# An expert's gate and up products in seven block products for eight, and its gathered rows moved inside the chip

## The chip, the cores and the metric

One core of a Trainium2 chip runs the whole program. The time is the device time of one execution, in microseconds. Three runs of the kernel before took 678.39 to 678.44 us, with a median of 678.43. TensorE (PE) multiplies matrices, VectorE (DVE), ScalarE (ACT) and GpSimd (POOL) work on elements, SyncE (SP) issues most transfers, and POOL issues the indirect ones. PEld is the loading of weights into PE.

## The reference

A layer on 8 sequences of 256 tokens with 512 features, in float32. An attention in the form of a long convolution comes first; the change does not touch it. Then each of the 2048 tokens chooses 4 of 16 experts, and every expert works on at most 256 tokens:

```python
xg = xpad[buf]                                   # 16 experts x 256 tokens x 512
gact = silu(einsum('ech,ehi->eci', xg, w_gate))  # 512 -> 352
mid = gact * einsum('ech,ehi->eci', xg, w_up)
eout = einsum('eci,eih->ech', mid, w_down) * wbuf[..., None]
y = zeros((T + 1, h)).at[buf.reshape(-1)].add(eout.reshape(-1, h))[:T]
shared = silu(x @ sw_gate) * (x @ sw_up) @ sw_down
x + y + shared
```

## The kernel before, in words

The first 340 us hold the attention, with the shared expert's blocks filled in between (`shared_block`, L142 to L197); the rest of these blocks runs until 419 us, while the routing is worked out. From there on the loop over the 16 experts has PE to itself. Constants: P = 128, NC = 4 chunks of the 512 features, CAP = 256 tokens in NSL = 2 halves of 128, NB = 4 blocks of 32, I = 352 = 2 x 128 + 96, so NW = 2 whole feature tiles and a tail of 96. AHEAD = 3 is how many experts the loop looks ahead.

Every engine works through its instructions in the order of the program (a manual schedule); nothing is moved by a planner. Semaphores hold the dependences between engines. For expert e the loop issues:

- `gate_up` (L1023): first the tail. Its gate and up columns lie packed in `wt`; L1046 and L1054 multiply them with the tokens `xgT`, and three rounds of an ACT operation (L1063 twice, L1067) and a DVE multiplication (L1064 twice, L1068) give its part of `mid`. These rounds use one tile in turn, so ACT and DVE alternate. Then for each of the two whole feature tiles f, gate and up with 4 chunks each: 16 products with 256 tokens as columns (L1034) in all. ACT takes the silu of gate out of PSUM (L1041), DVE multiplies by up from PSUM (L1042).
- `pack(e+1)` (L1011), two copies on ACT, and `tokens(e+1)` (L998): two copies of the routing weights (L1003) and two block transposes of 32 x 32 (L404) on DVE. They turn the rows in `gb` into `xgT`, features on the partitions.
- `find(e+3)` (L915): PE finds the expert's tokens from the comparison made earlier (L920), and seven small DVE operations (L928 to L943) form the index lists. Then `gather(e+3)` (L974): two indirect transfers on POOL (L977) fetch 256 rows into `g`.
- `down` (L1076) for n = 0 and n = 1: six products (tail, f = 0, f = 1, of both halves; L1080 at 512 columns), DVE scales the result by the routing weight on its way out of PSUM (L1088), and POOL adds the rows to `out` with an indirect transfer (L1091), after a small memset (L1090).
- `compare(e+4)` (L904): one DVE comparison of 2048 elements a partition, with both inputs in SBUF (L907).
- `load_expert(e+3)` (L852): four transfers on SP, 2.2 MB of weights, into the buffers that expert e leaves. Then `shuffle(e+3)` (L985): the gathered rows are written to a DRAM tile `slots` (L989), and four transfers of 32 partitions each read them back as `gb` (L992), in the order that the block transposes want: partition b of block i holds the features of block i, of the rows b of every block j.

Expert 15 is done in halves of 128 tokens, so that its first half can leave while the second is multiplied. `xnT` (L103, 32 KB a partition) holds the normalised tokens for the shared expert; after the last shared block nothing reads it. `ps_mm` and `ps_tr` are the PSUM pools of that part, two buffers each, free in the expert loop; the loop's own pool `ps_ex` has three.

Of the kernel before, what the change touches and what calls it, by code (L numbers as in the profile page):

```python
# [8 lines left out]
F32 = mybir.dt.float32  # L9
BF16 = mybir.dt.bfloat16  # L10
I32 = mybir.dt.int32
AF = mybir.ActivationFunctionType
# [8 lines left out]
P = 128  # L21
BK = 32
B, S, L = 8, 256, 512
# [7 lines left out]
E, K, CAP, I, IS = 16, 4, 256, 352, 704  # L31
NSL = CAP // P
NB = P // BK
# [20 lines left out]
def ssm_attention__then__moe_kernel(  # L54
# [22 lines left out]
    nc = tc.nc  # L77
# [25 lines left out]
    xnT = keep.tile([P, NC, NT, P], F32, name="xnT")  # L103
# [156 lines left out]
    with ExitStack() as att:  # L260
# [16 lines left out]
            out=exch,  # L277
            in_=exch,
# [386 lines left out]
        def stir(count):  # L665
# [7 lines left out]
            out=skip_b,  # L673
            in_=bass.AP(tensor=skip.tensor, offset=skip.offset + FIRST * HT, ap=[[0, P], [1, HT]]),
# [164 lines left out]
    ffn = ctx.enter_context(tc.tile_pool(name="ffn", bufs=2))  # L839
# [6 lines left out]
    AHEAD = 3  # L846
# [5 lines left out]
    def load_expert(e):  # L852
        if e % AHEAD < AHEAD - 1:
            w = wpool.tile([P, 2, NC, I], F32, name="w")
            wd = wpool.tile([P, NI, L], F32, name="wd")
        else:
            w, wd = old_w, old_wd
        full = I // P * P
        nc.sync.dma_start(out=w[:, 0], in_=w_gate[e].rearrange("(p c) f -> p c f", p=P))
        nc.sync.dma_start(out=w[:, 1], in_=w_up[e].rearrange("(p c) f -> p c f", p=P))  # L860
        nc.sync.dma_start(
            out=wd[:, 0 : I // P, :], in_=w_down[e, 0:full, :].rearrange("(c p) f -> p c f", p=P)
        )
        nc.sync.dma_start(out=wd[0 : I - full, I // P, :], in_=w_down[e, full:, :])
        return w, wd
# [79 lines left out]
    experts = {e: load_expert(e) for e in range(AHEAD)}  # L945
# [39 lines left out]
    def shuffle(g):  # L985


        slots = dram.tile([CAP, L], F32, name="slots", bufs=2)
        nc.sync.dma_start(out=slots.rearrange("(n q) f -> q n f", n=NSL), in_=g[:, :, 0:L])  # L989
        gb = ffn.tile([P, NSL * NB, P], F32, name="gb", bufs=AHEAD - 1)  # L990
        for i in range(NB):
            nc.sync.dma_start(  # L992
                out=gb[i * BK : (i + 1) * BK],
                in_=slots[:, i * P : (i + 1) * P].rearrange("(j b) f -> b j f", b=BK),
            )
        return gb

    def tokens(e):  # L998

        gb, g = moved.pop(e), gathered.pop(e)  # L1000
        wg = ffn.tile([P, NSL], F32, name="wg")
        for n in range(NSL):
            nc.vector.tensor_copy(wg[:, n : n + 1], g[:, n, L + e : L + e + 1])  # L1003
        xgT = ffn.tile([P, NC, CAP], F32, name="xgT")
        for n in range(NSL):
            transpose_blocks(xgT[:, :, n * P : (n + 1) * P], gb[:, n * NB : (n + 1) * NB])
        return xgT, wg

    NW, Q = I // P, P // 4
# [13 lines left out]
    def gate_up(xgT, mid, w, wt, cols, fs=(I // P, *range(I // P))):  # L1023

        halves = range(cols.start // P, cols.stop // P)
        for f in fs:
            pgu = ps_ex.tile([P, 2, CAP], F32, name="pgu", tag="ex")
            act = ffn.tile([P, CAP], F32, name="eact")  # L1030
            if f < NW:
                for k in range(2):
                    for c in range(NC):
                        nc.tensor.matmul(  # L1034
                            pgu[:, k, cols],
                            lhsT=w[:, k, c, f * P : (f + 1) * P],
                            rhs=xgT[:, c, cols],
                            start=(c == 0),
                            stop=(c == NC - 1),
                        )  # L1040
                nc.scalar.activation(act[:, cols], pgu[:, 0, cols], AF.Silu)  # L1041
                nc.vector.tensor_mul(mid[:, f, cols], act[:, cols], pgu[:, 1, cols])  # L1042
                continue
            for c in range(NC):
                for n in halves:
                    nc.tensor.matmul(  # L1046
                        pgu[2 * Q * n : 2 * Q * (n + 1), 1, 0:P],
                        lhsT=wt[:, c, P:],
                        rhs=xgT[:, c, n * P : (n + 1) * P],
                        start=(c == 0),  # L1050
                        stop=(c == NC - 1),
                    )
            for c in range(NC):
                nc.tensor.matmul(  # L1054
                    pgu[:, 0, cols],
                    lhsT=wt[:, c, 0:P],
                    rhs=xgT[:, c, cols],
                    start=(c == 0),
                    stop=(c == NC - 1),
                )  # L1060
# [12 lines left out]
    between = route.tile([P, 1], F32, name="between")  # L1073
    SYNC = mybir.DependencyInfo(mybir.DependencyClass.Sync, mybir.DependencyReason.DATA)

    def down(e, n, mid, wd, wg):  # L1076
        po = ps_ex.tile([P, L], F32, name="eo", tag="ex")
        for k, f in enumerate((NW, *range(NW))):
            m = min(P, I - f * P)
            nc.tensor.matmul(  # L1080
                po,
                lhsT=mid[:m, f, n * P : (n + 1) * P],
                rhs=wd[:m, f, :],
                start=(k == 0),
                stop=(k == NW),
            )
# [12 lines left out]

        done = done.ins  # L1100
        scattered.append(done)
        if e > 0:
            if n == 1:
# [9 lines left out]
    xgT_next = tokens(0)  # L1113
# [5 lines left out]
    for e in range(E):  # L1119
        w, wd = experts.pop(e)  # L1120
        wt = wt_next
        xgT, wg = xgT_next
        mid = ffn.tile([P, NI, CAP], F32, name="mid")
        if e + 1 < E:
            gate_up(xgT, mid, w, wt, slice(0, CAP))
            wt_next = pack(experts[e + 1][0])
            xgT_next = tokens(e + 1)
            if e + AHEAD < E:
                find(e + AHEAD, hots.pop(e + AHEAD))
                gathered[e + AHEAD] = gather(e + AHEAD)  # L1130
            for n in range(NSL):
                down(e, n, mid, wd, wg)
            if e + AHEAD + 1 < E:
                hots[e + AHEAD + 1] = compare(e + AHEAD + 1)
        else:

            gate_up(xgT, mid, w, wt, slice(0, P))
            gate_up(xgT, mid, w, wt, slice(P, CAP), (NW,))
            down(e, 0, mid, wd, wg)
            gate_up(xgT, mid, w, wt, slice(P, CAP), range(NW))  # L1140
            down(e, 1, mid, wd, wg)
        if e + AHEAD < E:
            experts[e + AHEAD] = load_expert(e + AHEAD)
            moved[e + AHEAD] = shuffle(gathered[e + AHEAD])
# [38 lines left out]
```

## Time and profile before

| what | value |
|---|---|
| median of three runs | 678.43 us |
| the profiled execution | 678.52 us |
| its span | 676.8 us |
| granted PE clock over the span | 0.995 |
| PE busy | 654.2 us, 97% |
| PEld busy | 486.9 us, 72% |
| DVE busy | 385.8 us, 57% |
| POOL busy | 320.2 us, 47% |
| ACT busy | 184.2 us, 27% |
| 11 loads of `w` by gate, 11 by up, 5 and 5 into the old tile `xs` | 704 KB each |
| L1034, 256 columns, 480 instructions | 106.0 us busy, mean 379 ns |
| L907 comparison on DVE, 16 | 36.5 us busy, mean 2281 ns |
| L977 gathers on POOL, 32 | 34.9 us busy, mean 1092 ns |
| L1091 scatters on POOL, 32 | 59.5 us busy, mean 1859 ns |

A line of the timeline or of the chain has the start and the length in microseconds, the engine, the line of the kernel, the operation and its tiles, the shape and how many instructions were merged; in brackets stands how long the engine idled before it and what ended that. PE's instructions overlap their predecessor's, so the mean of one (379 ns) is longer than the distance to the next; what a product costs in a stream is read from start to start. A float32 product of the program is two PE instructions.

### The profile page before, as it was taken

Reading aid. Unit: us, or ns where it says so; the run is one execution under the profiler, and the core shown is the slowest. Engines: PE = TensorE matmul, PEld = TensorE weight load, DVE = VectorE, ACT = ScalarE, POOL = GpSimd, SP = SyncE. Lnnn points to the kernel's source line nnn. Section 1 sums busy time; section 2 is a strip of 40 time slices with the busy share of each in tenths; the row PEclk is TensorE's granted clock in tenths of the full one; section 3 lists DMA queues with packets and bytes.
Section 4 is the critical chain, followed back from the end, with each engine's and each line's share of the span. In section 5 each row is a group of like instructions: output and inputs, shape, how many; then the busy total and the mean of one; then the engine's idle time right before and its main releaser. Section 6 shows DMA issues by size and latency. Waiting matters only on the chain.

```text
span 676.8 us, 9807 instructions
## 1 busy us (share of the span) xinstructions
PE 654.2 (97%) x3321; PEld 486.9 (72%) x3321; DVE 385.8 (57%) x932; ACT 184.2 (27%) x465; POOL 320.2 (47%) x509
## 2 busy tenths in 40 slices
PE   6899999998999999999999999999999999999994
PEld 5687877777867877876867685777776667777772
DVE  4956576878877776767536621444445545553231
ACT  2464533444342343313332010111121111111110
POOL 5677646877685777547120320243333444443111
PEclk9999999999999999999999999999999999999998
DMA  5793455555557536351008672588888889999822
GB/s 131 237 269 105 125 151 145 145 140 140 147 141 188 134 94 161 103 133 46 16 23 298 198 234 64 169 267 255 259 269 269 256 258 270 271 266 273 248 32 31
DMA packets 98439, 117.79 MB, mean 174 GB/s; under 512 B 11268, under 2 KB 64356, under 8 KB 98389
## 3 DMA queue, kind: packets, MB, share of 16 engines
q1 hardware_dynamic: 90932, 99.86, 48.9%
q0 software_dynamic: 7168, 17.04, 12.1%
q10 hardware_dynamic: 288, 0.26, 0.3%
q8 instruction: 26, 0.43, 0.3%
q14 instruction: 25, 0.20, 0.1%
HBM read 84.25 MB, written 32.88 MB: 173 GB/s over the span
## 4 chain that ended last, share of the span: by engine, by line
PE 85%; DVE 4%; DMA 3%; issue 2%; POOL 2%; ACT 2%; SPq 1%; POOLq 0%; DVEq 0%; ACTq 0%
PE sgu L168 20%; PE pgu L1034 15%; PE y L468 15%; PE eo L1080 12%; PE so L185 11%; PE pgu L1054 4%; PE pgu L1046 2%; PE sgt L154 2%; PE shared L468 2%; PE ip L920 1%; PE pt L529 1%; POOL kv L445 1%; DMA xs<-in_x 1%; DMA out<-eo_sb,idx 1%; DVE y L517 1%
## 5 line engine op out<-in xcount | busy, mean ns | idle before, releaser
L468 PE MATMUL y<-kv,toep 128*128 128x288 f32 x528 | 138.7, 407 | 4.8 <-DVE f L518 3.0
L468 PEld LDWEIGHTS y<-kv,toep 128*128 128x128 f32 x528 | 98.9, 190 | 35.4 <-issue 7.1
L977 POOL DMA_INDIRECT g<-xw_d,ido x32 | 34.9, 1092 | 170.8 <-DVE idx L943 132.3
L520 POOL TENSOR_TENSOR f<-f 128x256 f32<-128x256 f32 x60 | 43.8, 730 | 90.2 <-DVE f L518 85.0
L445 POOL TENSOR_TENSOR kv<-k 128x256 f32<-128x256 f32 x126 | 85.1, 707 | 0.0
L1091 POOL DMA_INDIRECT out<-eo_sb,idx x32 | 59.5, 1859 | 46.1 <-DVE eo_sb L1088 35.4
L168 PE MATMUL sgu<-xnT,swg 128*128 128x256 f32 (+1 forms) x400 | 78.1, 338 | 0.4 <-DVE tail L162 0.4
L1034 PE MATMUL pgu<-xgT,w 128*128 128x256 f32 (+1 forms) x384 | 78.2, 362 | 0.0
L168 PE MATMUL sgu<-xnT,swu 128*128 128x256 f32 (+1 forms) x400 | 77.9, 338 | 0.0
L1034 PEld LDWEIGHTS pgu<-xgT,w 128*128 128x128 f32 x384 | 68.2, 190 | 8.7 <-issue 0.5
L185 PE MATMUL so<-swd,smid 128*128 128x512 f32 x160 | 73.9, 593 | 0.0
L168 PEld LDWEIGHTS sgu<-xnT,swg 128*128 128x128 f32 x400 | 65.3, 191 | 7.9 <-DVE tail L162 0.6
L168 PEld LDWEIGHTS sgu<-xnT,swu 128*128 128x128 f32 x400 | 64.6, 191 | 6.3
L1080 PE MATMUL eo<-wd,mid 96*128 96x512 f32 (+1 forms) x132 | 59.4, 598 | 0.0
L1042 DVE TENSOR_TENSOR mid<-eact,pgu 128x256 f32<-128x256 f32 (+1 forms) x34 | 13.8, 406 | 77.6 <-ACT eact L1041 77.6
L491 DVE TENSOR_TENSOR y<-y,again 128x576 f32<-128x576 f32 x28 | 21.4, 766 | 57.8 <-PE y L468 48.1
L185 PEld LDWEIGHTS so<-swd,smid 128*128 128x128 f32 x160 | 29.9, 190 | 31.9 <-issue 30.4
L177 ACT ACTIVATE act<-sgu 128x256 f32<-128x256 f32 (+1 forms) x50 | 17.1, 341 | 121.6 <-PE sgu L168 121.6
L518 DVE TENSOR_TENSOR f<-y,z 128x512 f32<-128x512 f32 x64 | 44.3, 692 | 6.6 <-DVE y L517 0.5
L517 DVE TENSOR_TENSOR y<-y,q 128x512 f32<-128x512 f32 x64 | 44.8, 700 | 2.2
L1063 ACT ACTIVATE eact<-pgu 32x128 f32<-32x128 f32 x32 | 8.5, 267 | 129.0 <-PE pgu L1054 123.8
L1080 PEld LDWEIGHTS eo<-wd,mid 96*128 96x128 f32 (+1 forms) x132 | 24.1, 189 | 26.0 <-issue 23.5
(178 smaller groups left out, 928.2 us busy)
## 6 DMA issues: line engine op xcount, KB each, us to landing
toep<-win_d SPq DMA_DIRECT2D x28, 320.0 KB
slots<-g SPq DMA_DIRECT2D x16, 512.0 KB
gb<-slots SPq DMA_DIRECT2D x64, 128.0 KB
w<-in_L_ffn_w_gate SPq DMA_DIRECT2D x11, 704.0 KB
w<-in_L_ffn_w_up SPq DMA_DIRECT2D x11, 704.0 KB
got<-sent SPq DMA_DIRECT2D x26, 256.0 KB
wd<-in_L_ffn_w_down SPq DMA_DIRECT2D x11, 512.0 KB
xs<-in_x SPq DMA_DIRECT2D x16, 256.0 KB
```

Source lines behind the costliest of these rows:

```text
L168: nc.tensor.matmul(pgu[:, k, :], lhsT=sw[:, c, f * P : (f + 1) * P], rhs=toks[:, c, :], start=(c == 0), stop=(c == NC - 1),)
L185: nc.tensor.matmul(po, lhsT=m[:, i * P : (i + 1) * P], rhs=swd[:, (f - 1) % (NF + 1), :], start=(f == 0), stop=(f == NF),)
L445: (nc.vector if c in helped else nc.gpsimd).tensor_mul(kv[:, c, 0 : ND * HB].rearrange("p (d w) -> p d w", d=ND), kh[:, c, 0:HB].unsqueeze ...
L468: nc.tensor.matmul(out, lhsT=toep[:, m * P : (m + 1) * P], rhs=rhs, start=(n == 0), stop=(n == len(pairs) - 1),)
L517: nc.vector.tensor_mul(yd, yd, view(qq, 0, [[qc, 2], [B, ND], [1, HB]]))
L518: nc.vector.tensor_add(f, yd, z[:, :, :, BACK : BACK + HB])
L520: adder.tensor_add(f[:, :, 0:2, :], f[:, :, 0:2, :], f[:, :, 2:4, :])
L977: nc.gpsimd.indirect_dma_start(out=g[:, n, :], out_offset=None, in_=xw_d[:, :], in_offset=bass.IndirectOffsetOnAxis(ap=ido[:, e, n : n + 1 ...
L1034: nc.tensor.matmul(pgu[:, k, cols], lhsT=w[:, k, c, f * P : (f + 1) * P], rhs=xgT[:, c, cols], start=(c == 0), stop=(c == NC - 1),)
L1054: nc.tensor.matmul(pgu[:, 0, cols], lhsT=wt[:, c, 0:P], rhs=xgT[:, c, cols], start=(c == 0), stop=(c == NC - 1),)
L1080: nc.tensor.matmul(po, lhsT=mid[:m, f, n * P : (n + 1) * P], rhs=wd[:m, f, :], start=(k == 0), stop=(k == NW),)
L1091: done = nc.gpsimd.indirect_dma_start(out=out, out_offset=bass.IndirectOffsetOnAxis(ap=idx[:, e, n : n + 1], axis=0), in_=o, in_offset=Non ...
```

## The change

`shuffle` no longer goes through DRAM. Sixteen transfers from SBUF to SBUF, one for each pair of a block j of rows and a block i of features, bring the rows from `g` to `gb`, whose layout gets the halves on the outside.

For experts 1 to 14 the two whole feature tiles of gate and up are no longer multiplied in the plain way. The 512 features are halved into k = 0, 1 (two chunks each), the outputs into gate and up, the 256 tokens into two halves of 128. In these 2 x 2 x 2 blocks the plain way has eight block products; `strassen` forms seven, of 8 instructions with 128 columns each for a block of two feature tiles and two chunks (7 x 2 x 2 = 28 products, 56 PE instructions, for 16 products and 32 instructions with 256 columns). What it needs besides:

- `weight_sums(e+1)`: four POOL operations of 512 elements a partition on the next expert's weights, at the head of iteration e.
- `token_sums(e+1)`: four DVE operations of 256 elements on the next expert's tokens, behind `tokens(e+1)`.
- In `strassen`: two ACT copies out of PSUM and two silu operations, and seven DVE operations: two additions into `u2` and two into `u3` with one input in PSUM, one addition and two multiplications with both inputs in SBUF.

The sums and intermediate results lie in `xnT`, two sets for two experts. Four PSUM tiles of `ps_mm` and `ps_tr` take the products. The tail and expert 0 and 15 stay as they were. `down` takes the second half (n = 1) ahead of the first. The diff, cut to its core:

```diff
     def shuffle(g):
-        slots = dram.tile([CAP, L], F32, name="slots", bufs=2)
-        nc.sync.dma_start(out=slots.rearrange("(n q) f -> q n f", n=NSL), in_=g[:, :, 0:L])
-        gb = ffn.tile([P, NSL * NB, P], F32, name="gb", bufs=AHEAD - 1)
-        for i in range(NB):
-            nc.sync.dma_start(
-                out=gb[i * BK : (i + 1) * BK],
-                in_=slots[:, i * P : (i + 1) * P].rearrange("(j b) f -> b j f", b=BK),
-            )
+        gb = ffn.tile([P, NSL, NB, P], F32, name="gb", bufs=AHEAD - 1)
+        for j in range(NB):
+            for i in range(NB):
+                nc.sync.dma_start(
+                    out=gb[i * BK : (i + 1) * BK, :, j, :],
+                    in_=g[j * BK : (j + 1) * BK, :, i * P : (i + 1) * P],
+                )
         return gb
...
+    def weight_sums(e, w):
+        (a11, a12), (a21, a22) = blocks_of(w)
...
+        nc.gpsimd.tensor_add(sums[0], a21, a22)
+        nc.gpsimd.tensor_sub(sums[1], sums[0], a11)
+        nc.gpsimd.tensor_sub(sums[2], a11, a21)
+        nc.gpsimd.tensor_sub(sums[3], a12, sums[1])
+        return sums
+
+    def token_sums(e, xgT):
...
+        nc.vector.tensor_sub(sums[0], b12, b11)
+        nc.vector.tensor_sub(sums[1], b22, sums[0])
+        nc.vector.tensor_sub(sums[2], b22, b12)
+        nc.vector.tensor_sub(sums[3], b21, sums[1])
+        return sums
+
+    def strassen(xgT, mid, w, s, t):
...
+        product(0, a11, b11)
+        nc.scalar.copy(p1, ps[0])
+        product(1, s[1], t[1])
+        nc.vector.tensor_add(u2, ps[1], p1)
+        product(2, s[0], t[0])
+        nc.scalar.copy(p5, ps[2])
+        product(0, a12, b21)
+        nc.scalar.activation(act0, ps[0], AF.Silu)
+        product(2, s[3], b22)
+        nc.vector.tensor_add(u2, ps[2], u2)
+        nc.scalar.activation(act1, u2, AF.Silu)
+        product(1, s[2], t[2])
+        nc.vector.tensor_add(u3, ps[1], p1)
+        nc.vector.tensor_add(p5, u3, p5)
+        nc.vector.tensor_mul(mid[:, 0:NW, P : 2 * P], act1, p5)
+        product(3, a22, t[3])
+        nc.vector.tensor_add(u3, ps[3], u3)
+        nc.vector.tensor_mul(mid[:, 0:NW, 0:P], act0, u3)
...
         mid = ffn.tile([P, NI, CAP], F32, name="mid")
+        if e + 2 < E:
+            s_next = weight_sums(e + 1, experts[e + 1][0])
         if e + 1 < E:
-            gate_up(xgT, mid, w, wt, slice(0, CAP))
+            if e == 0:
+                gate_up(xgT, mid, w, wt, slice(0, CAP))
+            else:
+                gate_up(xgT, mid, w, wt, slice(0, CAP), (NW,))
+                strassen(xgT, mid, w, sums, token_sums_now)
             wt_next = pack(experts[e + 1][0])
             xgT_next = tokens(e + 1)
+            if e + 2 < E:
+                sums, token_sums_now = s_next, token_sums(e + 1, xgT_next[0])
             if e + AHEAD < E:
                 find(e + AHEAD, hots.pop(e + AHEAD))
                 gathered[e + AHEAD] = gather(e + AHEAD)
-            for n in range(NSL):
+            for n in reversed(range(NSL)):
                 down(e, n, mid, wd, wg)
```

Products 0 and 3 of the second round add to what the same PSUM tile already holds. In the changed kernel the product is at L1132, the POOL sums at L1095 to L1098, the token sums at L1111 to L1114, ACT's copies at L1147 and L1151, DVE's operations at L1149, L1155, L1158, L1159, L1160, L1162 and L1163, and the down products at L1169.

More of the change, by code (lines that the diff above doesn't have):

```diff
@@ L1005, in tokens @@
         for n in range(NSL):
-            transpose_blocks(xgT[:, :, n * P : (n + 1) * P], gb[:, n * NB : (n + 1) * NB])
+            transpose_blocks(xgT[:, :, n * P : (n + 1) * P], gb[:, n])
         return xgT, wg
@@ L1074, in ssm_attention__then__moe_kernel, with spare, blocks_of @@
     SYNC = mybir.DependencyInfo(mybir.DependencyClass.Sync, mybir.DependencyReason.DATA)
+    F = NW * P
+    free = xnT.rearrange("p c n q -> p (c n q)")
+    def spare(at, n):
+        return free[:, at : at + n]
+    def blocks_of(w):
+        return [[w[:, m, 2 * k : 2 * k + 2, 0:F] for k in range(2)] for m in range(2)]
+    def weight_sums(e, w):
+        (a11, a12), (a21, a22) = blocks_of(w)
+        sums = [
+            spare((e % 2 * 4 + i) * 2 * F, 2 * F).rearrange("p (c f) -> p c f", c=2)
+            for i in range(4)
+        ]
+        nc.gpsimd.tensor_add(sums[0], a21, a22)
[3 more added lines that the diff above has]
+        return sums
@@ new lines, in token_sums @@
+    def token_sums(e, xgT):
+        (b11, b12), (b21, b22) = [
+            [xgT[:, 2 * k : 2 * k + 2, n * P : (n + 1) * P] for n in range(2)] for k in range(2)
+        ]
+        at = 16 * F
+        sums = [
+            spare(at + (e % 2 * 4 + i) * 2 * P, 2 * P).rearrange("p (c q) -> p c q", c=2)
+            for i in range(4)
+        ]
+        nc.vector.tensor_sub(sums[0], b12, b11)
[3 more added lines that the diff above has]
+        return sums
@@ new lines, in strassen, with product, place @@
+    def strassen(xgT, mid, w, s, t):
+        (a11, a12), (a21, a22) = blocks_of(w)
+        (b11, b12), (b21, b22) = [
+            [xgT[:, 2 * k : 2 * k + 2, n * P : (n + 1) * P] for n in range(2)] for k in range(2)
+        ]
+        ps = [
+            pool.tile([P, NW, P], F32, name=f"gu{i}", tag=tag)
+            for i, (pool, tag) in enumerate(((ps_mm, "mm"), (ps_mm, "mm"), (ps_tr, "pt"), (ps_tr, "pt")))
+        ]
+        begun = set()
+        def product(i, a, b):
+            for f in range(NW):
+                for c in range(2):
+                    nc.tensor.matmul(
+                        ps[i][:, f, :],
+                        lhsT=a[:, c, f * P : (f + 1) * P],
+                        rhs=b[:, c, :],
+                        start=(i not in begun),
+                        stop=(c == 1),
+                        skip_group_check=True,
+                    )
+                    begun.add(i)
+        def place(i):
+            return spare(16 * F + 16 * P + i * F, F).rearrange("p (f q) -> p f q", f=NW)
+        p1, p5, u2, u3, act0, act1 = (place(i) for i in range(6))
+        product(0, a11, b11)
[16 more added lines that the diff above has]
+        nc.vector.tensor_mul(mid[:, 0:NW, 0:P], act0, u3)
@@ L1102, in down @@
         if e > 0:
-            if n == 1:
+            if len(scattered) % 2 == 0:
                 tc.declare_no_dep(done, scattered[2 * e], reason="other rows of out")
```

## The prediction

> **What bounds the kernel now.** I read the chain of work first. Its shares by engine and by line:
>
> ```profile
> PE 85%; DVE 4%; DMA 3%; issue 2%; POOL 2%; ACT 2%; SPq 1%; POOLq 0%; DVEq 0%; ACTq 0%
> PE sgu L168 20%; PE pgu L1034 15%; PE y L468 15%; PE eo L1080 12%; PE so L185 11%; PE pgu L1054 4%; PE pgu L1046 2%; PE sgt L154 2%; PE shared L468 2%; PE ip L920 1%; PE pt L529 1%; POOL kv L445 1%; DMA xs<-in_x 1%; DMA out<-eo_sb,idx 1%; DVE y L517 1%
> ```
>
> The change touches the expert loop, 419 us to the end. Next, the chain in order of time there (start, length, what), one expert:
>
> ```profile
> 512.30 1.02 PE pgu L1046 x16
> 513.32 1.92 PE pgu L1054 x8
> 515.25 6.91 PE pgu L1034 x32
> 522.15 0.38 PE ip L920 x16
> 522.53 5.26 PE eo L1080 x12
> ```
>
> 1.02 + 1.92 + 6.91 + 0.38 + 5.26 = 15.49 us per expert, and the next begins at 527.79: PE never waits. A matrix product of the program is two PE instructions (16 calls of L1034 are x32). Busy time in the stretch of eight such experts (PE, PEld, DVE, ACT, POOL, clock, DMA share, GB/s) shows what is near PE:
>
> ```profile
> 496.80:620.80 124.00, 124.00 (x674) 88.33 (x676) 61.08 (x152) 19.92 (x56) 49.65 (x48) 1.00 0.92 274
> ```
>
> Per expert DVE 7.6 us, POOL 6.2, ACT 2.5, so each has room by its mean. DVE's waits in the stretch are for PE or ACT, PE's for nothing.
>
> **PE's gain.** The timeline gives the price of both widths: 256 columns before, 128 in the last expert, which is cut in halves already.
>
> ```profile
> 515.08 7.07 PE L1034 MATMUL pgu<-xgT,w 128*128 128x256 f32 x32
> 521.99 0.54 PE L920 MATMUL ip<-what,hot 128*128 128x6 bf16 x16
> ...
> 661.01 3.73 PE L1034 MATMUL pgu<-xgT,w 128*128 128x128 f32 x32
> 664.58 2.74 PE L1080 MATMUL eo<-wd,mid 96*128 96x512 f32 x6
> ```
>
> From start to next start, (521.99 - 515.08)/32 = 0.216 us and (664.58 - 661.01)/32 = 0.1116 us. Seven products of 8 instructions are 56 x 0.1116 = 6.25 us for 6.91: 0.66 less. Experts 1 to 14 take the new way, so 14 x 0.66 = 9.2 us if PE goes on unhindered, at 14.84 us per expert.
>
> **DVE's chain without collisions.** DVE gains five operations in the products (seven, L1149 to L1163, in place of the two multiplications L1042; the tail's three stay: 5 x 0.42 = 2.1 us) and four token sums (L960, same size, both inputs in SBUF: 0.424; 1.6 us together). They form a ring, since DVE runs in order and the next expert's PE needs it back:
> - From the sixth product in PSUM: add, add, multiply, add, multiply, 2.1; copies of the weights and two transposes, 1.34 (538.53 to 539.86 before); token sums 1.6; the seven small index operations 1.0; two evictions 1.34; the comparison L907 2.2. Together 9.6.
> - Then the next tail: three multiplications alternating with ACT, then ACT's copy of p1, which the fourth product waits for because it writes the same PSUM: 0.28 + 0.31 + 0.32 + 0.42 + 0.38 + 0.19 to PE = 1.9.
> - Products four to six: 3 x 0.894, and 0.2 until DVE sees them: 2.9.
>
> 14.4 us, under PE's 14.84. So this alone hides, with 0.4 us of slack.
>
> **POOL's sums and the shared port.** POOL gets four operations of 512 elements per expert. L520 and L521 on POOL (adds) took 0.730 us for 256 elements and 0.459 for 128, 2.12 ns an element, so 512 are about 1.28 us. The multiplications L445 and L443 give 1.2 as the low bound; 1.4 is the high one (strided operands). Mean time allows 5.1 us: POOL 6.2 + 5.1 of 15. But the trace shows what DVE operations with both inputs in SBUF do beside such work. At 32 us POOL idles, at 15 us it multiplies:
>
> ```profile
> 15.22 0.72 DVE L520 TENSOR_TENSOR f<-f 128x256 f32<-128x256 f32 x1
> 15.61 0.89 POOL L445 TENSOR_TENSOR kv<-k 128x256 f32<-128x256 f32 x1
> 15.97 0.67 DVE L521 TENSOR_TENSOR oT<-f 128x128 f32<-128x128 f32 x1
> ...
> 32.28 0.42 DVE L520 TENSOR_TENSOR f<-f 128x256 f32<-128x256 f32 x1
> 32.74 0.29 DVE L521 TENSOR_TENSOR oT<-f 128x128 f32<-128x128 f32 x1
> ```
>
> L521 took 0.67 for 0.29: it ends 0.29 after 16.35, and POOL ended at 16.50. POOL's own 0.89 for 0.70 is the same the other way. They take turns, each beginning about 0.14 before the other's end. The Trainium skill (SBUF — State Buffer, Who interferes with whom) has the rule: a DVE instruction with two SBUF inputs and a GpSimd instruction that reads SBUF exclude each other for the whole instruction; one with a PSUM input does not. The row agrees except for those 0.14 us of overlap; L518 (one input in PSUM) stays at 692 ns beside a busy POOL. POOL's indirect transfers are held too, by the comparison:
>
> ```profile
> 381.89 2.28 DVE L907 TENSOR_TENSOR hot<-pos,slot_f 128x2048 bf16<-128x2048 f32 x1
> 382.77 2.50 POOL L977 DMA_INDIRECT g<-xw_d,ido  x1 [27.72 <-DMA xw_d<-prob]
> 385.57 0.97 POOL L977 DMA_INDIRECT g<-xw_d,ido  x1 [0.30 <-issue]
> ```
>
> **Where they meet.** POOL's order is gather, gather, scatter, scatter, four sums for the expert after the next. The first gather goes when DVE has the index; the second is held by the comparison and ends 1.1 us after it; 0.3 + 1.93 + 1.6 for the scatters: the sums begin about 4.9 us after the comparison's end. DVE's first add of two SBUF operands (into p5) wants to begin 1.9 + 2.9 + 0.45 = 5.25 after the same end. So it finds the first sum 0.35 us old and waits 1.28 - 0.35 - 0.14 = 0.8. The second sum takes the port as it ends; the multiplication behind it waits 1.28 - 0.31 = 0.95; the last multiplication comes 0.37 after that one and waits 0.6; the fourth sum falls beside the transposes, which have one input (705 ns where POOL is busy, 686 here). The waits are 2.35 us, the ring is 14.4 + 2.35 = 16.8. PE feels it twice: the down product of the second half waits for its mid, and the fourth product for p1. Who else is queued: the gathers behind the sums have 6 us and more before a transfer is missed. By the rule without the 0.14 the waits are 0.7 longer and the end 11 x 0.7 = 8 us later (700); I take the row.
>
> Sum: experts 2 to 12, 11 x (16.78 - 15.50) = +14.1; expert 1 about even (its ring begins undelayed), -0.1; expert 13, with no comparison behind it but sums still to come, +0.95; expert 14, no sums, -0.65. Together +14.3. The profiled execution took 678.52 us (span 676.8; the 1.7 around it stay), the median of the runs is 678.43: 678.5 + 14.3 = 692.8.
>
> **The direct transfers.** The write of 512 KB to DRAM goes, and five issues become sixteen. SP waited 73.4 us in eight experts for the write to land, yet nobody waited for SP: one wait of 1.5 us for gb in all. So I cost it at nothing. 16 x 0.45 (four gb issues took 1.80) + 1.7 for the weights = 8.9 us of SP per expert, under 15; the next weights are queued behind, needed more than an expert later. Packets are 512 bytes as in the reads before. Low bound 0 gain, since no wait is there to go; high bound, if gb came an expert's slack (6 us at the last one) too late, some us once. The reversed order of the halves (its first half is the one finished first), the first expert's unchanged products and the PE waits for sums on hand a whole expert ahead cost nothing while the ring lets them.
>
> **Rivals.**
> - The exclusion hardly bites (sums shorter, or falling into DVE's other work): 678.5 - 9.2 = 669.3, faster. It decides from waits under 15.5 - 14.4 = 1.1 us per expert. For it: POOL is free 9 of 15 us. Against: the sums follow the same comparison as DVE's adds, so the phase repeats. 10%.
> - Half of it: POOL's transfers are not held as I think, or an operation costs 1.0: one or two waits remain, ring 14.9 to 15.8, 672 to 683. 13%.
> - Worse: sums of 1.4 us and more, token sums caught too, or gb late: 699 to 710. 5%.
> - The forecast: 683 to 698 with its bounds (1.2 us per sum +10.7, 1.4 +19), 72%.
>
> The measurement can tell about 0.2% (1.4 us). Faster: 10 and most of half of the 13, 0.17; same 0.04; slower 0.79. The range leaves out the clean gain, the lower part of the half case and the worst: 678 to 699.
>
> **What would show it.** Right: L1132 at 112 ns from start to start; PE idle before it and before eo, ended by ACT or DVE; the DVE lines L1159, L1160 and L1163 at 0.8 to 1.4 us for 0.42; POOL sums at 1.28 and more; experts 16.8 us apart. Wrong: those DVE lines at 0.42 and experts 14.84 apart, or waits for gb or w on PE.

## The result and the profile after

The changed kernel took 698.04 us, the median of four runs (696.66 to 698.61), against 678.43 before: 1.0286 times as long, with an interval of 1.0274 to 1.0299. The profiled execution took 696.66 us, with a span of 694.9. Two ratios further down, 0.9963 and 1.0074, are formed without those executions of their kernel that lie over 1.5% above its fastest one, while the medians are over all of them.

First the chain of work of the kernel after, its shares by engine (SPq is SP's issuing of transfers). PE carried 85% before:

```profile
PE 53%; DMA 16%; SPq 10%; DVE 8%; POOL 5%; issue 4%; ACT 2%; POOLq 0%; DVEq 0%; ACTq 0%
```

Busy time in a stretch of some seven experts of it (stretch, its length, PE, PEld, DVE, ACT, POOL, clock, DMA share, GB/s):

```profile
520.00:640.00 120.00, 109.83 (x779) 80.89 (x774) 95.49 (x202) 21.36 (x63) 92.19 (x72) 1.00 0.87 224
```

PE had no idle moment in such a stretch before and has 10 us here; DVE has gone from 49% of the stretch to 80%, POOL from 40% to 77%. An operation that is held counts as busy, so these shares contain waits. One expert of it, on PE:

```profile
503.15 1.09 PE L1045 MATMUL pgu<-xgT,wt 128*64 128x128 f32 x16
...
506.00 1.05 PE L1132 MATMUL gu<-xgT,xs 128*128 128x128 f32 x8
506.89 1.95 PE L1132 MATMUL gu<-xnT 128*128 128x128 f32 x16
509.13 1.16 PE L1132 MATMUL gu<-xgT,xs 128*128 128x128 f32 x8 [0.28 <-issue]
...
515.20 4.56 PE L1169 MATMUL eo<-xs,mid 128*128 128x512 f32 x10 [0.89 <-DVE mid L1160]
519.69 1.09 PE L1045 MATMUL pgu<-xgT,wt 128*64 128x128 f32 x16
```

A block product of 8 instructions takes 0.89 us (506.00 to 506.89), 0.111 each. The saving is there. But the next expert begins 16.54 us after this one, and 15.50 was the distance before. PE stands before the down product of the second half until DVE has made `mid` (L1160), and for a shorter time before the fourth product, which begins 2.24 us after two products of 0.89 (506.89 to 509.13), 0.45 late. DVE's and POOL's lines of the same expert show why:

```profile
505.18 2.28 DVE L907 TENSOR_TENSOR hot<-pos,slot_f 128x2048 bf16<-128x2048 f32 x1
...
512.11 0.42 DVE L1158 TENSOR_TENSOR xnT<-gu,xnT 128x256 f32<-128x256 f32 x1
512.57 1.17 DVE L1159 TENSOR_TENSOR xnT<-xnT 128x256 f32<-128x256 f32 x1
513.84 1.30 DVE L1160 TENSOR_TENSOR mid<-xnT 128x256 f32<-128x256 f32 x1
...
515.51 1.05 DVE L1163 TENSOR_TENSOR mid<-xnT 128x256 f32<-128x256 f32 x1
```

```profile
505.26 3.05 POOL L977 DMA_INDIRECT g<-xw_d,ido  x1 [0.30 <-issue]
...
511.60 1.85 POOL L1095 TENSOR_TENSOR xnT<-w 128x512 f32<-128x512 f32 x1
513.53 1.33 POOL L1096 TENSOR_TENSOR xnT<-xnT,w 128x512 f32<-128x512 f32 x1
514.83 1.46 POOL L1097 TENSOR_TENSOR xnT<-w 128x512 f32<-128x512 f32 x1
```

Operations of one size: the one with `gu` (PSUM) among the inputs takes 0.42, those with both inputs in `xnT` 1.05 to 1.30. Each of the three ends 0.27 to 0.29 after a POOL sum has ended (L1159 at 513.74, L1095 at 513.45), so it begins 0.14 before that end and has waited until then: 0.75, 0.88 and 0.63 us. Behind L1163, which waits for the third sum, DVE has the transposes with one input while the fourth sum runs, and the token sums after it take 0.42 each.

SP's queue in the same kernel, from one expert's direct transfers to the next one's loads (start, length with the waits inside, how many):

```profile
514.97 14.35 SPq L991 DMA_DIRECT2D gb<-g  x16
529.49 0.49 SPq L859 DMA_DIRECT2D xs<-in_L_ffn_w_gate  x1
...
546.23 0.49 SPq L859 DMA_DIRECT2D w<-in_L_ffn_w_gate  x1
```

From load to load it is 16.7 us here (529.49 to 546.23), and 15.7 to 18.3 us between the other loads from 493 us on, with SP hardly idle. So a second limit may stand as close as the first. It is not a fixed price: the first two groups of sixteen in the loop took 10.3 and 10.2 us. In the later groups SP stands between its issues, by the profile most often until weights have landed (26 us from 420 to 680 us).

Where the 18.1 us of span went: 1.6 before the loop (it starts at 420.83, at 419.24 before); experts 1 to 12 at 1.03 more than 15.50 each, 12.4; 2.8 more in single ones of these (expert 2 0.84, expert 12 1.36); expert 13 2.0 more; expert 14 0.6 less.

### The profile page after: what moved, and what is told of

The parts are those of the page before. It is cut to its first block, busy times and chain, and to the rows that moved or that the text cites. A ratio compares the mean times of both kernels' runs of the same rounds, so it can differ in the third digit from the quotient of the medians.

```text
span 694.9 us, 11010 instructions
## 1 busy us (share of the span) xinstructions
PE 653.0 (94%) x3657; PEld 490.8 (71%) x3657; DVE 464.3 (67%) x1058; ACT 192.2 (28%) x493; POOL 411.4 (59%) x565
## 4 chain that ended last, share of the span: by engine, by line
PE 53%; DMA 16%; SPq 10%; DVE 8%; POOL 5%; issue 4%; ACT 2%; POOLq 0%; DVEq 0%; ACTq 0%
PE sgu L168 18%; PE y L468 14%; PE so L185 10%; SPq L991 8%; DMA xs<-in_L_ffn_w_down 3%; DMA wd<-in_L_ffn_w_down 3%; DMA g<-xw_d,ido 3%; DMA gb<-g 2%; PE gu L1132 2%; DMA w<-in_L_ffn_w_up 2%; PE eo L1169 2%; POOL g L977 2%; PE shared L468 2%; PE sgt L154 1%; POOL out L1180 1%
## 5 line engine op out<-in xcount | busy, mean ns | idle before, releaser
L977 POOL DMA_INDIRECT g<-xw_d,ido x32 | 58.0, 1811 | 104.3 <-DVE idx L943 52.7
L1180 POOL DMA_INDIRECT out<-eo_sb,idx x32 | 52.2, 1631 | 37.2 <-DVE eo_sb L1177 28.3
L1169 PE MATMUL eo<-wd,mid 96*128 96x512 f32 (+1 forms) x132 | 61.8, 605 | 8.8 <-DVE mid L1160 8.8
L1169 PEld LDWEIGHTS eo<-wd,mid 96*128 96x128 f32 (+1 forms) x132 | 23.3, 189 | 37.8 <-issue 19.4
L1132 PE MATMUL gu<-xnT 128*128 128x128 f32 x336 | 42.1, 275 | 0.0
L1132 PEld LDWEIGHTS gu<-xnT 128*128 128x128 f32 x336 | 39.8, 192 | 0.0
L907 DVE TENSOR_TENSOR hot<-pos,slot_f 128x2048 bf16<-128x2048 f32 x16 | 36.5, 2281 | 0.0
```

The source lines that it names most:

```text
L977: nc.gpsimd.indirect_dma_start(out=g[:, n, :], out_offset=None, in_=xw_d[:, :], in_offset=bass.IndirectOffsetOnAxis(ap=ido[:, e, n : n + 1 ...
L1132: nc.tensor.matmul(ps[i][:, f, :], lhsT=a[:, c, f * P : (f + 1) * P], rhs=b[:, c, :], start=(i not in begun), stop=(c == 1), skip_group_ch ...
L1169: nc.tensor.matmul(po, lhsT=mid[:m, f, n * P : (n + 1) * P], rhs=wd[:m, f, :], start=(k == 0), stop=(k == NW),)
L1180: done = nc.gpsimd.indirect_dma_start(out=out, out_offset=bass.IndirectOffsetOnAxis(ap=idx[:, e, n : n + 1], axis=0), in_=o, in_offset=Non ...
```

## The experiments

Two theories. P: POOL's weight sums and DVE's operations with two SBUF inputs take turns on a port, and this sets 16.5 us an expert. S: the direct transfers on SP, behind which the next weights queue, set it, and the collisions lie in their shadow. The unchanged kernel took 678.3 to 678.4 us beside every group of runs.

**1. The rows through DRAM again.**

```diff
-        gb = ffn.tile([P, NSL, NB, P], ...)
-        for j in range(NB):
-            for i in range(NB):
-                nc.sync.dma_start(out=gb[i*BK:(i+1)*BK, :, j, :], in_=g[j*BK:(j+1)*BK, :, i*P:(i+1)*P])
+        nc.sync.dma_start(out=slots..., in_=g[:, :, 0:L])          # as before the change
+        for i in range(NB):
+            nc.sync.dma_start(out=gb[i*BK:(i+1)*BK], in_=slots[...])
```

> The changed kernel with the rows going through DRAM again (one write, four reads), so without the sixteen direct transfers. Theory P (the POOL sums and DVE's operations with two SBUF inputs exclude each other and set 16.5 us per expert; the direct transfers only add their lateness, 1.6 us before the loop and about 4 in five of the experts): 691 to 693. Rival S (the sixteen issues of SP, 0.64 us each, and the waits between them form a ring of 17 us which sets the pace): experts fall under 15.5 us and the time under 676.

Measured: 692.86 us, 1.021 (1.0193 to 1.0227). The loop begins at 418.99, and experts 3 to 12 stand 16.52 to 16.55 apart, all of them, with the same waits as in the changed kernel:

```profile
528.69 1.16 DVE L1160 TENSOR_TENSOR xnT<-xnT 128x256 f32<-128x256 f32 x1
529.95 1.30 DVE L1161 TENSOR_TENSOR mid<-xnT 128x256 f32<-128x256 f32 x1
```

So S does not set the distance of the clean experts; P does so alone. Expert 2 took 20.3 here. In the first round POOL's second scatter waited 4.42 us, the weight sums came late (444.70 to 450.6), and they met the last multiplication (2.16 us) and two token sums; PE then stood 2.72 us before the fourth product. A clean expert takes 16.54, so this round costs 3.8 us. The direct transfers cost the rest, 698.04 - 692.86 = 5.2 us, in a kernel that is slow enough to hide most of them.

**2. The direct transfers alone**, in the kernel before (its `gate_up` and `down` unchanged, `shuffle` as in the change).

> The kernel before with the direct transfers alone, no block products. Theory P: DVE has 6 us of slack per expert, so only the 1.6 us before the loop and perhaps one late row transfer: 680 to 682. Rival S: experts are drawn out from 15.5 towards 17 us once the two experts of lead are used up, 686 to 697.

Measured: 679.93 us, 1.0019 (1.0011 to 1.0027). Every expert of the loop stands at 15.50 as before; the loop begins at 420.84, 1.6 us late. PE's wait before the loop, 1.39 us in this run, is the one that the changed kernel has (1.59 in brackets, in the changed kernel's line):

```profile
403.42 1.99 PE L168 MATMUL sgu<-xnT,swg 128*128 128x256 f32 x8 [1.59 <-DVE smid L179]
```

DVE stood there before its first transposes of `gb`, which the sixteen transfers bring later than the five did; its multiplication for the shared expert (L179) is queued behind them. At 15.50 us an expert the direct transfers are hidden from then on. SP took 19 us from load to load at first, and 14.8 to 16.2 from 523 us on. Sixteen direct transfers and four loads lie between these two:

```profile
554.24 0.52 SPq L859 DMA_DIRECT2D w<-in_L_ffn_w_gate  x1
...
569.00 0.52 SPq L859 DMA_DIRECT2D xs<-in_L_ffn_w_gate  x1
```

So the 16.7 us of the changed kernel is not a floor of SP's queue.

**3. No weight sums from expert 3 on**, direct transfers kept. The kernel leaves these sums out, so its output is not the reference's.

```diff
         sums = [spare(...) for i in range(4)]
+        if e > 2:
+            return sums
         nc.gpsimd.tensor_add(sums[0], a21, a22)
```

> The changed kernel with the POOL sums of weights left out from expert 3 on (the products then read the sums of experts 1 and 2, so the experts' results are not the reference's). Everything else as in the changed kernel, direct transfers too. Theory P: L1159, L1160 and L1163 fall to 0.42 us, no wait of PE for mid, experts at 14.84 to 14.9 us unless rows are late: 671 to 676. Rival S: the transfers keep the experts at 16 us and more: 688 to 697. If the two act together, DVE's three operations fall to 0.42 and the waits for gb grow by most of it.

Measured: 690.59 us, 1.0186 (1.0159 to 1.0212). The product operations fall to 0.42 us and experts 3 and 4 to 14.84 us. From then on experts take 15.9 to 17.6. Waits in that stretch (us in total, times, longest):

```profile
DVE xgT L404 <- DMA gb<-g: 19.8, 8, 3.4
```

Both theories have a part of the truth: the limits are stacked. Take P's away, and the direct transfers give nearly all of it back; run 4 shows how much.

**4. No weight sums from expert 3 on, and the rows through DRAM**: both edits above, and again sums left out.

> Rows through DRAM as before, the product form kept, the weight sums left out from expert 3 on (so the output is not the reference's). It tells what the product form is worth when neither POOL's sums nor the direct transfers are there. Theory (collisions first, the transfers' ring second): product operations of 0.42 us, experts 3 to 13 at 14.84 us, PE bound; from the run with rows through DRAM (692.9): 10 experts x 1.69 less, some 3 to 5 us less in expert 2 and 0.9 in expert 13, up to 4 us given back where the rows come late: 671 to 676 us. Rival (PE cannot run the 7 products faster than about 15.5, or DVE's ring of 14.4 us is the bound anyway): experts at 15.5 or more, 680 us or more. The same kernel with direct transfers took 690.6; the difference between the two is the price of the direct transfers once the collisions are gone.

Measured: 676.86 us (674.67 to 679.41), 0.998 (0.9971 to 0.9989). Experts 3 to 7 stand at 14.84 and the later ones at 14.84 to 16.67, with DVE waiting for `gb` by up to 2.7 us. Against run 3 the direct transfers cost 13.7 us. That is just above the 671 to 676 expected of P: expert 2 still took 17.83, and late rows account for the rest. Two stretches of this run:

```profile
468.59:527.96 59.37, 59.37 (x433) 45.16 (x432) 44.52 (x113) 12.62 (x36) 30.00 (x25) 1.00 0.91 266
527.96:605.10 77.14, 75.26 (x541) 56.74 (x540) 56.03 (x141) 15.57 (x45) 37.37 (x31) 1.00 0.90 273
```

In the first one PE is busy throughout, at 14.84 us an expert: PE can do it, and DVE's ring is no limit there.

**5. POOL writes the sums' tiles and reads nothing** (rows through DRAM; the values of the sums are left out). Each sum becomes three memsets of 512, 512 and 128 elements, about as long together as the sum.

```diff
-        nc.gpsimd.tensor_add(sums[0], a21, a22)      # and the three tensor_sub
+        for total in sums:
+            nc.gpsimd.memset(total, 0.0)
+            nc.gpsimd.memset(total, 0.0)
+            nc.gpsimd.memset(total[:, 0, 0:P], 0.0)
```

> Rows through DRAM; each of POOL's four sums is replaced by three memsets of the same output, 512, 512 and 128 elements, in the same place of POOL's order (the sums' values are left out, so the output is not the reference's). The semaphores, buffers and order stay. If the waits of DVE's product operations come from POOL reading SBUF (theory as first put: exclusion of reads), they vanish: 0.42 us each, experts at 14.84, about 672 to 676 us. If any POOL operation on SBUF excludes them, also one that only writes, waits remain, each at most as long as one memset: experts between 14.84 and 16.5, 676 to 690 us. If it is a semaphore or an order of instructions and not the port, nothing changes: 692.9 us.

Measured: 675.43 us, 0.9964 (0.995 to 0.9978). DVE and POOL at one time:

```profile
503.02 0.42 DVE L1160 TENSOR_TENSOR xnT<-xnT 128x256 f32<-128x256 f32 x1
```

```profile
502.66 0.53 POOL L1098 MEMSET xnT<- 128x512 f32 x1
503.24 0.21 POOL L1099 MEMSET xnT<- 128x128 f32 x1
```

POOL is as busy as with the sums and at the same time, and nobody waits. So it is neither POOL's being occupied nor an order of semaphores, but its reading of SBUF. That agrees with the Trainium skill (SBUF — State Buffer, Who interferes with whom): a DVE operation with two SBUF inputs contends with a GpSimd operation that reads SBUF, and not with one that only writes it. The lines of the kernel before could show the first half alone. The clean experts are at 14.84 us; late rows again take some.

**6. The same sums in eight halves** (rows through DRAM).

```diff
+        for c in range(2):
+            cut = slice(c, c + 1)
-        nc.gpsimd.tensor_add(sums[0], a21, a22)
+            nc.gpsimd.tensor_add(sums[0][:, cut], a21[:, cut], a22[:, cut])     # and so on
```

> Rows through DRAM; the same four sums in eight operations of 128x256 instead of four of 128x512. Collision theory: a product operation waits for the rest of the one POOL operation that runs, less an overlap of 0.14 us, so a wait is at most about 0.55 us instead of 1.15 (0.75, 0.88 and 0.63 measured); after it POOL is held for the 0.42 us. Experts at about 15.3 to 16.1, 681 to 689 us. Rival (POOL's whole run of sums is what DVE waits for): as before, 16.5 per expert and 692.9 us.

Measured: 688.98 us, 1.0159 (1.0142 to 1.0176). DVE in a clean expert:

```profile
527.83 0.76 DVE L1163 TENSOR_TENSOR mid<-xnT 128x256 f32<-128x256 f32 x1
...
530.84 0.99 DVE L1114 TENSOR_TENSOR xnT<-xgT 128x256 f32<-128x256 f32 x1
```

The part of theory P that was at stake holds: a wait is the rest of one POOL operation, now 0.18, 0.34 and 0.09 us in the products. The expected time (681 to 689) was met only at its end and the distance of 15.3 to 16.1 not at all, since experts still take 16.41: each half takes 0.72 to 0.92 us instead of half of 1.28, POOL's run of sums is longer, and it now reaches three token sums, which wait 0.57, 0.41 and 0.52. The loss moved along DVE's order.

**7. No product operation with two SBUF inputs** (rows through DRAM; full sums). The p5 tile goes to the free half of a PSUM bank, and the last sum u3 is written to PSUM.

```diff
-        p1, p5, u2, u3, act0, act1 = (place(i) for i in range(6))
+        p1, u2, u3, act0, act1 = (place(i) for i in range(5))
+        p5 = full[1][:, NW : 2 * NW, :]              # the tile gu1 is twice as large
...
-        nc.vector.tensor_add(u3, ps[3], u3)
-        nc.vector.tensor_mul(mid[:, 0:NW, 0:P], act0, u3)
+        nc.vector.tensor_add(ps[3], ps[3], u3)
+        nc.vector.tensor_mul(mid[:, 0:NW, 0:P], act0, ps[3])
```

> Rows through DRAM, all sums and products kept, but p5 and the last u3 lie in PSUM, so that none of DVE's operations of the products has two inputs in SBUF. Theory P: the three operations take 0.42 us beside the same POOL sums of 1.27 us, experts at 14.9, 669 to 672, faster than both kernels. If the exclusion did not depend on where the inputs lie: as e1_dram, about 692. If POOL's occupation itself (gathers and scatters behind the sums) cost the time: also about 692.

Measured: 680.61 us, 1.0033 (1.002 to 1.0045), 12 us less than run 1, but over the 669 to 672 expected. All product operations take 0.42 to 0.43 us beside running sums, but one of the token sums, still with two SBUF inputs, meets what is left of POOL's run:

```profile
524.51 0.42 DVE L1164 TENSOR_TENSOR mid<-xnT,gu 128x256 f32<-128x256 f32 x1
...
527.10 1.56 DVE L1112 TENSOR_TENSOR xnT<-xgT 128x256 f32<-128x256 f32 x1
```

```profile
527.11 1.27 POOL L1099 TENSOR_TENSOR xnT<-w,xnT 128x512 f32<-128x512 f32 x1
```

That wait of 1.1 us is enough for 15.5 to 15.7 us an expert, and expert 2 took 19.06.

**8. The mended kernel**: run 7, and the weight sums of expert e+2 are formed right after the gather of expert e and before its scatters, so that they are over before the token sums begin; the output rows `eo_sb` get four buffers for three.

```diff
+    s_next = weight_sums(1, experts[1][0])           # ahead of the loop
...
                 gathered[e + AHEAD] = gather(e + AHEAD)
+            if e + 3 < E:
+                s_next = weight_sums(e + 2, experts[e + 2][0])
             for n in reversed(range(NSL)):
                 down(e, n, mid, wd, wg)
```

> Rows through DRAM, product operations with one input each in PSUM, and the weight sums of expert e+2 formed right after the gather and before the scatters of expert e (output rows in four buffers), so that they end before the token sums begin. Theory: no DVE operation with two SBUF inputs stands beside a POOL sum any more, so all product operations and token sums take 0.42 us; experts 1 to 13 at 14.84 us, 0.66 less than before: 670 to 673 us, up to 675 if rows come late in places; faster than both kernels. Rival (another wait takes their place: scatters that come later hold the output rows, or rows through DRAM come late in every expert): experts at 15.5, 679 us or more.

Measured: 677.37 us, the median of 12 (669.81 to 681.33), 0.9963 (0.9941 to 0.9985). This is above the 670 to 675 expected. Every product operation and every token sum takes 0.41 to 0.43 us, the late round of expert 2 is gone, and experts 1 to 7 all stand at 14.84 us. The best single run, 669.81, comes near what PE's savings promise, 678.3 - 14 x 0.66 = 669.1. Most runs did not. The stretches of experts 3 to 6 and of experts 7 to 12 in the profiled execution (681.33 us):

```profile
464.35:523.72 59.37, 59.37 (x434) 45.16 (x433) 44.55 (x113) 12.55 (x36) 49.73 (x41) 1.00 0.97 272
523.72:620.48 96.76, 92.67 (x649) 69.95 (x648) 66.12 (x161) 18.82 (x54) 74.24 (x60) 0.98 0.86 257
```

In the first PE never waits and the DMA engines are at 0.97. Before the change they were at 0.92 with 15.50 us, from which I estimate 0.92 x 15.50 / 14.84 = 0.96 for the same work in 14.84. From expert 8 on the rows come late: `gb` by up to 4.9 us, six times, and experts take up to 18.99. Full engines alone do not account for it, since their share is 0.86 in this second stretch, and 0.90 in run 4 where rows were late too. The order on SP's queue is the other candidate. From 523 to 621 us SP waited for each write of rows to land before it could issue the read back, with the next loads behind it (us in total, times, longest). It waited so before the change too, 73.4 us in eight experts, but there it was hidden.

```profile
SPq L992 <- DMA slots<-g: 79.8, 7, 12.4
```

**9. Rows written to DRAM ahead of the next weights** in the mended kernel, to take the write out of SP's ring.

```diff
+            slots = shuffle(gathered[e + AHEAD])         # the write alone
             experts[e + AHEAD] = load_expert(e + AHEAD)
-            moved[e + AHEAD] = shuffle(gathered[e + AHEAD])
+            moved[e + AHEAD] = blocks(slots)             # the four reads
```

> The mended kernel of the run before (one PSUM input in each product operation, weight sums formed early, rows through DRAM), with one move on SP's queue: the write of an expert's rows to DRAM is issued before the next weight loads and not after them, the read back after the loads. In the run before, most experts took 14.84 us, but seven waited for rows, up to 4.9 us: SP issues the read back only when the write has landed, and the write lies behind 2.1 MB of weights (issued at 535.41, read back issued at 547.22); the next loads wait behind that on SP's queue, a ring of some 16 us. Theory (the ring of loads, write, read back sets the rest): the write is out of the ring, the waits for gb go, experts at 14.84 us throughout: 668 to 672 us, and the spread between runs shrinks. Rival (the DMA engines are full: 4.2 MB per expert, at 298 GB/s for a full share, worked out from 0.92 at 274 GB/s in the kernel before, are 14.1 us, and the bytes don't change): late rows remain, 674 to 678 us.

Measured: 679.66 us (678.13 to 683.69), 1.0022 (1.0007 to 1.0038). This is above the 668 to 672 of my theory and the 674 to 678 of its rival. The wait for the write went, but the write now waits for the gathered rows, with the loads behind it (SP's waits from 498 to 610 us):

```profile
SPq L989 <- DMA g<-xw_d,ido: 54.8, 7, 9.4
SPq L995 <- DMA slots<-g: 6.5, 7, 1.7
```

Experts 5 to 11:

```profile
498.49:610.13 111.64, 107.36 (x757) 80.13 (x756) 77.47 (x191) 21.95 (x63) 87.09 (x70) 1.00 0.97 268
```

An expert takes 15.95 us with the engines at 0.97. The packets add up to 15.5 us an expert here (0.97 x 15.95) and to 14.3 before (0.92 x 15.50), for the same bytes. That fits the rival, the full DMA engines, but does not show it: the edit moved SP's wait to another place and did not remove it. Why the packets took longer, the runs don't tell.

**10. The mended kernel with the direct transfers.**

> The same mended product form (one PSUM input, weight sums early), with the direct transfers of the change in place of the way through DRAM: what the change's second half does when the first no longer slows the experts. Theory: SP's 16 issues of 0.64 us and the landing of the weights make a ring of about 17 us, as in the run without sums; most experts from the fourth on wait for gb: 16 to 17 us per expert, loop 1.6 us later: 687 to 693 us, slower than before. Rival (fewer bytes leave the DMA engines room, the ring closes at 15 us or less): 671 to 677 us.

Measured: 705.41 us (701.85 to 709.32), 1.0381 (1.036 to 1.0403), more than I expected: experts 1 to 4 take 14.84, the later ones 17.1 to 20.2. The waits from 480 us on, and the busy time:

```profile
DVE xgT L404 <- DMA gb<-g: 43.2, 10, 7.0
```

```profile
500.00:680.00 180.00, 155.97 (x1011) 115.66 (x1009) 99.74 (x254) 30.64 (x88) 108.58 (x93) 0.95 0.75 195
```

The DMA engines stand at 0.75, so their room is not what is short here, and fewer bytes don't help. SP's sixteen issues took 15.9 to 17.2 us an expert (540 to 605 us), since SP stood between them, by the profile for weights that had to land (58 us in 34 waits from 480 to 690 us). Why its stream is longer than in run 3, the runs don't tell.

**11 and 12. The weight loads on ACT's queue**, in run 10 and in run 8, to break SP's ring.

```diff
-            experts[e + AHEAD] = load_expert(e + AHEAD)
+            experts[e + AHEAD] = load_expert(e + AHEAD, nc.scalar)
```

> The mended product form with direct transfers (705.4), and one move: the four weight loads of an expert are issued on ACT's DMA queue, at the start of the next expert, where ACT stands idle before L1066's kind of activation, and no longer on SP's queue behind the 16 direct transfers. It tells whether the ring of issues on SP (16 direct transfers that wait for the landing of weights, then the next loads) set the 705.4, or the DMA engines themselves. Theory (the ring): loads start when the buffers are free, the direct transfers wait for the gather alone; experts at 14.84 us, loop 1.6 us later than before: 670 to 675 us. Rival (DMA engines full or the direct transfers' packets too slow beside weights): experts at 16 us or more, 688 us or more. ACT pays some 2 us of issues per expert in its idle time.

> The same move of the weight loads to ACT's queue with rows through DRAM (677.4 with the loads on SP). Theory (ring of loads, write and read back): experts at 14.84 us but for a few late rows, 668 to 673 us. Rival (the DMA engines are the bound here: 57.2 us of 16 engines' packets for four experts, 14.3 us each in the mended kernel with the loads on SP, share 0.94 to 0.99 in the run with the writes first): late rows in every other expert stay, 675 to 680 us; the direct version is then the better of the two, since it moves half a megabyte less per expert.

Measured: 709.27 us, 1.0455 (1.0436 to 1.0473), with the direct transfers, and 685.41 us (679.33 to 690.12), 1.0074 (1.0046 to 1.0101), through DRAM. The first lies in its rival's range (688 or more), the second in neither range. The runs do not tell what they were made to tell, because the edit makes a new wait. ACT of the first one:

```profile
535.40 0.33 ACTq L859 DMA_DIRECT2D w<-in_L_ffn_w_gate  x1
544.44 0.33 ACTq L860 DMA_DIRECT2D w<-in_L_ffn_w_up  x1
...
545.87 0.27 ACT L1062 ACTIVATE eact<-pgu 32x128 f32<-32x128 f32 x1 [12.17 <-PE gu L1132]
```

ACT stood 9 us between its first and second issue, and the activations of the expert behind them; PE then waited for ACT's copy of p1 by 3 to 5 us in every second expert. SP meanwhile issued 53 direct transfers without a pause for a load, in 54.15 us:

```profile
530.91 54.15 SPq L991 DMA_DIRECT2D gb<-g  x53
```

That is 1.02 us each, but it does not tell whether sixteen fit into 14.84 us: for 13.1 us of it SP stood waiting for gathered rows, in three waits, and in run 2 sixteen with four loads took 14.76. What an issue on ACT waits for, I can't say from the trace.

## Why the prediction was right, and where it was not

The forecast was 692.8 us, slower, for the collisions on the port. The direction, the place and the mechanism hold; the total (698.0) is 5.2 us higher, in the range but near its upper end.

- **PE's gain.** 0.111 us an instruction, and 14.84 us an expert wherever nothing stands in the way (runs 4, 5, 8): right.
- **DVE's ring of 14.4 us without collisions.** Runs 4, 5 and 8 show 14.84 with PE never idle, so it is at or under PE's time: right. In run 1 it is 16.53 - 2.26 = 14.3 without the waits.
- **The sums.** 1.27 to 1.29 us where nothing holds them, for 1.28.
- **The waits of 0.8, 0.95 and 0.6.** They were 0.75, 0.88 and 0.63. The sum began about 4.7 us after the comparison's end by its effective start (513.45 - 1.28 - 507.46) for 4.9. The overlap of 0.14, which I took from the lines of the kernel before where the rule has the whole instruction, recurs in all three.
- **The ring of 16.8.** 16.53 in run 1, so 0.25 too long: the waits were 2.26 together and not 2.35, and the way from the comparison's end to the fourth product took 1.67 us (507.46 to 509.13) and not 1.9. Over 11 experts this is 2.8 us too much.
- **Expert 1 about even, expert 2 like the others.** Wrong. In run 1 expert 1 gains its 0.66 in full, but expert 2 takes 4.8 us more than before, since the first round's scatters are late and push the sums into token sums. I had not followed POOL's queue through the start of the loop. The two errors nearly cancel: run 1, the product form without the direct transfers, lies 14.5 us above the kernel before, and my sum was +14.3. That it comes so close is luck.
- **The direct transfers at nothing.** This is the step that failed: "16 x 0.45 (four gb issues took 1.80) + 1.7 for the weights = 8.9 us of SP per expert, under 15". An issue took 0.64 us from start to start, 10.2 for the sixteen. Between issues SP stood up to 2.6 us more at a time, and with the loads its stream is 15.7 to 18.3 us in the changed kernel. I took the price from reads out of DRAM, and I looked at whether anybody waited for SP and not at whether SP's order would still close in time. In the changed kernel it costs 5.2 us between the medians and 3.7 between the profiled spans (694.9 and 691.2). Of these 3.7, 1.8 lie before the loop, 2.1 in experts 8, 9 and 12, whose rows came late, and 1.2 in expert 13, where the trace shows no wait for rows; experts 1 and 2 took 1.4 less than in run 1. Experts of 16.5 us hide the rest. In run 3, without the collisions, it costs 13.7.
- **The rivals.** The clean gain of 669.3 was reached by a single run of the mended kernel. That it was not the median has to do with late rows at 14.84 us an expert; I had late rows only within a rival of 5%, for another time. The DMA engines have little room there (0.96 by the estimate of run 8), and the order on SP's queue is the other candidate. Which of the two it is stays open.

## What to carry to other kernels

A saving on the bound engine is paid out only down to the next limit, so work out the second and the third before the edit: here the port (16.5 us), SP's queue with the direct transfers (experts of 15.9 to 17.6 in run 3) and late rows at 14.84 stood in a row, and PE waited for none of them in the profile before. When element work is added beside a stream of DVE operations, find out which of these have both inputs in SBUF; an input in PSUM, or an earlier place in POOL's order, took the waits to zero. A transfer that becomes many small ones is counted by its issues on their queue, at the price of that kind of transfer, and by what the queue waits for between them.

## What the runs showed of the hardware

- Issues of 32 KB from SBUF to SBUF took 0.59 us with a gap of 0.05, while four reads of 128 KB from DRAM took 1.80 together.
- An addition on POOL of 256 elements took 0.72 us at the least, one of 512 1.26 to 1.29: two small ones cost some 0.17 us more than one large one.
- A POOL memset of 512 elements took 0.53 us beside DVE operations with two SBUF inputs, and neither waited.
- An indirect gather that takes 0.97 us alone took 3.05 beside the comparison L907 (two inputs in SBUF), in nearly every expert of the changed kernel.
